# A mixture-of-experts kernel: each place gets a room of tokens in steps of 4 beside its slots in steps of 32

## The chip, the cores and the metric

The kernel runs on one core of one Trainium2 chip. The metric is the time on the device in microseconds (us); less is better. The engines are called as the profile calls them: PE is TensorE's matmul stream and PEld its weight loads, DVE is VectorE, ACT is ScalarE, POOL is GpSimd, SP is SyncE, whose queue issues most of the plain DMAs. L1387 is line 1387 of the kernel before.

## The reference, cut to what matters

There are 16 x 128 = 2048 tokens of width 512. The kernel computes one attention block and one mixture-of-experts block, each with a layer norm ahead and a residual behind. The change is in the second:

```python
x = x + xattn(layernorm(x), ctx, ctx)
h = layernorm(x).reshape(2048, 512)
tidx, tw = gate(h, gate_weight, e_bias)      # 8 of 32 experts for each token, and their weights
comb = zeros(2048, 32).at[rows, tidx].set(tw)
g = einsum('td,eid->tei', h, w1)             # up products, 256 wide per expert
u = einsum('td,eid->tei', h, w3)
a = silu(g) * u
routed = einsum('tei,edi,te->td', a, w2, comb)
shared = (silu(h @ sw1.T) * (h @ sw3.T)) @ sw2.T
out = x + routed + shared
```

The 2048 x 8 = 16384 pairs of a token and an expert are not spread evenly over the experts, and which tokens go where is known only on the chip.

## The kernel before

All products are in fp32; each of the program's matmuls on fp32 data shows as two MATMUL instructions in the profile. The work goes through three stages.

**Attention** (`attention_small`, until about 130 us) ends with the layer norm, the rows of normalized tokens in DRAM (`rows`) and the gate's logits.

**Routing** (`route`, then `slot_tokens`, until about 232 us) picks eight experts per token on DVE, counts the tokens of each expert, and gives each expert a rank by its count (rank 0 has most). Beside it PE computes the shared expert (L250, L1269). Each rank owns a *place*, a fixed stretch of slots of the length `CAPS[rank]`, in steps of 32 slots: 704 for rank 0 down to 448 for rank 31, 17664 slots in all, that is 138 slices of 128. `ORDER` says which rank's place comes at which position, `begins` where each place starts. A token's slot is the place's beginning plus its running number among the expert's tokens, which matmuls on fp16 zeros and ones add up in PSUM (`rank`). Where a place begins and how long it is enter these matmuls as differences to the neighbouring rank: `rise`, made on DVE at L1122 and L1125 from a small table `ranked` that POOL's memsets fill, is multiplied with `behind`, a 32 x 32 table of which rank is ahead of which. From this come `end_p` (L1192), `cap` (L1195) and `limit` (L1211); a token beyond its place's `limit` gets no slot. `flags` compares the counts with the lengths of the places and sets `more` if any expert has more tokens than its place takes. In that case, after the normal work, `rest()` runs every expert over all tokens and adds what was left out.

**Experts** (from about 232 us to the end) works through the 32 places in the order of their positions. A place with more than 512 slots, and the first and last place, is cut into two *pieces*; there are 52. For each piece PE computes the up products (`up`, L1387): two halves of the 256 rows, two weights (w1 and w3), four chunks of the 512 inputs, so 16 products over as many columns as the piece has slots. ACT applies silu (L1396) and DVE the product (L1398) into `acts` (`sa` in the profile). For each slice of 128 slots,

- `gather` (L1351, POOL) fetches the token rows from `rows` with an indirect DMA, five slices ahead,
- `turn` transposes them on PE (L1365), copies them on ACT to `xnT` (L1367), and picks the weights on DVE (L1372),
- `down` multiplies with w2 on PE (L1441), and ACT scales the result into `yw` (L1450),
- `send` (L1413, POOL) adds the rows to the output with an indirect DMA; slots without a token have a number out of bounds and are left out. The first `send` of a place waits until the last one of the place before has landed.

The order on PE, DVE, ACT and POOL is the order of the program, written out by hand: a piece has four steps of up products, and turns and downs of other slices lie between them. The weights of a place (three loads of 512 KB on SP's queue) are in one of three buffers, and are loaded once the place that used the buffer before is done.

The width of an up product is set in `up`:

```python
k, first, end = pieces[n]
m = end - first
```

Of the kernel before, what the change touches and what calls it, by code (L numbers as in the profile page):

```python
# [10 lines left out]
F16 = mybir.dt.float16  # L11
I32 = mybir.dt.int32
AF = mybir.ActivationFunctionType
ALU = mybir.AluOpType
# [4 lines left out]
P = 128  # L19
# [7 lines left out]
TOPK = 8  # L27
NW = 3


CAPS = (
    [704, 672] + [640] * 3 + [608] * 6 + [576] + [544] * 6 + [512] * 7 + [480] * 5 + [448] * 2
# [2 lines left out]
ORDER = [18, 0, 11, 1, 29, 2, 3, 4]  # L35
ORDER += [r for k in range(6) for r in (5 + k, 12 + k)]
ORDER += [*range(19, 29), 30, 31]
BIG = 32768
# [5 lines left out]
def tile_xattn_moe(  # L44
# [15 lines left out]
    nc = tc.nc  # L60
    B, S, D = x.shape
    E, _, ND, I = w1.shape
# [7 lines left out]
    begins = [sum(CAPS[r] for r in ORDER[:k]) for k in range(E + 1)]  # L70
# [71 lines left out]
    not_small = const.tile([1, 1], I32, name="not_small")  # L142
# [7 lines left out]
    limit = const.tile([P, E], F32, name="limit")  # L150

    more = const.tile([1, 1], I32, name="more")
# [802 lines left out]
    def experts(ups, in_order, later, products):  # L955
# [15 lines left out]
        ranked = wp.tile([E, 2, E + 1], F32, name="ranked")  # L971
        rank_at = wp.tile([E, E], F32, name="rank_at")
        for k in range(E + 1):
            r = min(k, E - 1)
            nc.gpsimd.memset(ranked[:, 0, k : k + 1], float(begin_of[r]))
            nc.gpsimd.memset(ranked[:, 1, k : k + 1], float(CAPS[r]))
        for k in range(E):
            nc.gpsimd.memset(rank_at[:, k : k + 1], float(ORDER[k]))

# [46 lines left out]
        def up_matmuls(n):  # L1026
            for _ in range(n):
                next(matmuls, None)

        def route():  # L1030
# [4 lines left out]
            def new(shape, name, dtype=F32, home=None):  # L1035
                return rt.tile(shape, dtype, tag=home or name, name=name)
# [64 lines left out]
            for t in range(NT):  # L1101
                nc.vector.max(t8[:, t, :], ms[:, t, :])
                nc.vector.match_replace(rp[:, t, :], t8[:, t, :], ms[:, t, :], LOWEST)
                if t == NT // 2:
                    product1()
                if t == NT // 2 + 1:


                    ranked_p = new([E, 4], "ranked_p")
                    diag = new([E, E], "diag")  # L1110
                    for i in range(4):
                        nc.vector.scalar_tensor_tensor(
                            diag,
                            ranked[:, i // 2, i % 2 : i % 2 + E],
                            1.0,
                            ident[0:E, 0:E],
                            ALU.mult,
                            ALU.mult,
                            accum_out=ranked_p[:, i : i + 1],
                        )  # L1120
                    rise = new([E, 3], "rise", F16)
                    nc.vector.tensor_tensor(  # L1122
                        rise[:, 0:2], ranked_p[:, 1::2], ranked_p[:, 0::2], ALU.subtract
                    )
                    nc.vector.tensor_tensor(rise[:, 2:3], rise[:, 0:1], rise[:, 1:2], ALU.add)  # L1125
            sel = new([P, NT, E], "sel", F16)
            nc.vector.tensor_tensor(sel, rp, ms, ALU.is_lt)
            comb = new([P, NT, E], "sf")
# [5 lines left out]
            for b in range(NT):  # L1134
                nc.tensor.matmul(
                    count_p,
                    lhsT=sel[:, b, :],
                    rhs=ones[:, 0:1],
                    start=(b == 0),
                    stop=(b == NT - 1),  # L1140
                )
            for b in range(NT):
                nc.tensor.matmul(
                    count,
                    lhsT=ones,
                    rhs=sel[:, b, :],
                    start=(b == 0),
                    stop=(b == NT - 1),
# [17 lines left out]
            for b in range(NT - 1):  # L1166
                nc.tensor.matmul(
                    rank[:, b + 1 :, :],
                    lhsT=ones,
                    rhs=sel[:, b : b + 1, :].to_broadcast([P, NT - 1 - b, E]),  # L1170
                    start=False,
                    stop=False,
                )
                if b == 3:
# [4 lines left out]
                        place, lhsT=ones[0:E, 0:E], rhs=less, start=True, stop=True  # L1179
                    )  # L1180
            behind = new([E, E], "behind", F16)
# [4 lines left out]
                lhsT=rise[:, 0:1].to_broadcast([E, P]),  # L1186
                rhs=behind.unsqueeze(1).to_broadcast([E, NT, E]),
                start=False,
                stop=True,
            )  # L1190
            end_p, cap = small2[:, E : 2 * E], small2[:, 2 * E : 3 * E]
            nc.tensor.matmul(  # L1192
                end_p, lhsT=rise[:, 2:3].to_broadcast([E, P]), rhs=behind, start=True, stop=True
            )
            nc.tensor.matmul(  # L1195
                cap, lhsT=rise[:, 1:2].to_broadcast([E, P]), rhs=behind, start=True, stop=True
            )
# [10 lines left out]
            owner_p = small2[:, 3 * E : 4 * E]  # L1208
            nc.tensor.matmul(owner_p, lhsT=expert_p, rhs=here, start=True, stop=True)
            up_matmuls(4)  # L1210
            nc.vector.tensor_scalar(limit, end_p, float(CAPS[0] - BIG), None, ALU.add)  # L1211
            own = new([P, NT, E], "own", F16, home="eq")
            nc.vector.tensor_tensor(
                own, rank, limit.unsqueeze(1).to_broadcast([P, NT, E]), ALU.is_lt
# [24 lines left out]
            def flags():  # L1239

                over = new([1, E], "over")
                nc.vector.tensor_copy(over, count[0:1])
                nc.vector.tensor_tensor(over, over, cap[0:1], ALU.subtract)
                most = new([1, 1], "most")
                nc.vector.tensor_reduce(most, over, AX.X, ALU.max)
                nc.vector.scalar_tensor_tensor(
                    more, most, float(CAPS[0]), not_small, ALU.is_gt, ALU.max
                )
                nc.vector.tensor_tensor(owner2, owner[:, 1:], owner[:, : E - 1], ALU.subtract)
                nc.vector.tensor_tensor(owner2, owner2, in_next, ALU.mult)  # L1250
                nc.vector.tensor_tensor(owner2, owner2, owner[:, : E - 1], ALU.add)
# [26 lines left out]
        def add_down(b, y):  # L1278
            nc.vector.tensor_tensor(xs[b], y, xs[b], ALU.add)
            nc.sync.dma_start(out[b], xs[b])  # L1280

        sr, sq, weights, flags = route()
        downs = iter(range(B))
        held = []
# [46 lines left out]
        for k in range(E):  # L1331
            first, end = begins[k], begins[k + 1]
# [46 lines left out]
                )  # L1379

        def up(n, i, w, banks):
            k, first, end = pieces[n]
            m = end - first
            pool = (ps_gu, ps_gu2)[i]
            acc = banks[w] = pool.tile([P, TB], F32, tag="gu", name="gu")
            for d in range(ND):
                nc.tensor.matmul(  # L1387
                    acc[:, 0:m],
                    lhsT=wup[k % NW][:, w, d, ts(i, P)],
                    rhs=xnT[n % NTB][:, d, 0:m],  # L1390
                    start=(d == 0),
                    stop=(d == ND - 1),
                )
            if w == 0:
                banks[2] = tp.tile([P, TB], F32, tag="sl", name="sl")
                nc.scalar.activation(banks[2][:, 0:m], acc[:, 0:m], AF.Silu)  # L1396
            else:
                nc.vector.tensor_tensor(  # L1398
                    acts[n % NTB][:, i, 0:m], banks[2][:, 0:m], acc[:, 0:m], ALU.mult
                )  # L1400
# [85 lines left out]
        for n in range(len(pieces)):  # L1486
            tasks = []
            whole = slices_of(n - 1)[1] if n else 0
            needed = slices_of(n + 1)[0] if n + 1 < len(pieces) else NS
            downs_left = list(range(n_down, whole))  # L1490
            turns_left = needed - n_turned
            n_down = whole
            banks = {}
            for step in range(4):
                up(n, step // 2, step % 2, banks)
                left = 4 - step
                for _ in range(-(-turns_left // left)):
                    turn_next()
                    turns_left -= 1
                for _ in range(-(-len(downs_left) // left)):  # L1500
                    down(downs_left.pop(0))
# [7 lines left out]
    pieces = [(k, i) for k in range(NTB) for i in range(NI)]  # L1509
    left_over = attention_small()  # L1510
    experts(pieces[1:], in_order, *left_over)
    left = nc.values_load(
        more[0:1, 0:1],
# [63 lines left out]
```

## Time and profile before

| | |
|---|---|
| median of 3 runs | 1022.8 us (1021.6 to 1024.35) |
| the profiled execution | 1022.55 us, its span 1020.8 us |
| PE busy | 996.8 us, 98% of the span |
| ACT, DVE, POOL busy | 326.2, 254.3, 513.1 us |
| up products (L1387) | 1664 MATMULs, first at 232.6 us |
| down products (L1441) | 672 MATMULs, 260.1 us busy |
| transposes (L1365) | 552 MATMULs, 82.9 us busy |
| granted TensorE clock | 0.995 |
| data moved | 137.06 MB, 134 GB/s in the mean |

The profile is one execution, recorded by the hardware. Matmuls overlap in PE's pipeline, so that the duration of one is longer than the time from its start to the start of the next; what a product costs a busy PE is read from starts. Idle time of an engine that doesn't set the pace costs nothing. A row of a group reads: line, engine, operation, output <- inputs, shapes and count, then busy us and mean ns of one, then the engine's idle time before it and what ended that.

### The profile page before, as it was taken

What the parts mean: (1) busy time and instruction counts of PE and PEld (TensorE: products, weight loads), DVE (VectorE), ACT (ScalarE), POOL (GpSimd) and SP (SyncE); (2) the same over time, 40 slices, a digit from 0 to 9 for tenths busy, and PEclk for the clock granted to TensorE, in tenths of its full rate; (3) what the DMA queues carried; (4) which work ended last, traced back from release to release, by engine and by line L of the source; (5) the groups of instructions that cost most, each with busy time, mean ns of one, the idle gap of its engine ahead of it and who ended that gap; (6) DMA issues with size and microseconds to landing.
All of it is one profiled execution on the core that took longest, in us unless ns stands there. A gap on an engine that the chain in (4) does not pass through costs nothing.

```text
span 1020.8 us, 12451 instructions
## 1 busy us (share of the span) xinstructions
PE 996.8 (98%) x4176; PEld 574.3 (56%) x4176; DVE 254.3 (25%) x902; ACT 326.2 (32%) x517; POOL 513.1 (50%) x658
## 2 busy tenths in 40 slices
PE   8999998999999999999999999999999999999996
PEld 5344444547566556676767676666654444444453
DVE  8887668961011001011111111111111000101000
ACT  5666612422322232232323232323222222222221
POOL 5588633754445444454545454545463444455443
PEclk9999999999999999999999999999999999999998
DMA  9011104135656657775757575757575767565633
GB/s 306 8 43 53 53 22 185 53 112 163 154 137 151 155 133 164 165 164 126 186 126 186 125 185 125 184 127 181 131 176 121 167 173 172 138 146 139 125 66 45
DMA packets 59864, 137.06 MB, mean 134 GB/s; under 512 B 12168, under 2 KB 16392, under 8 KB 59792
## 3 DMA queue, kind: packets, MB, share of 16 engines
q0 software_dynamic: 32032, 69.25, 35.5%
q1 hardware_dynamic: 27680, 66.81, 19.4%
q8 instruction: 35, 0.57, 0.2%
q14 instruction: 37, 0.30, 0.1%
q10 hardware_dynamic: 80, 0.13, 0.0%
HBM read 96.71 MB, written 46.73 MB: 141 GB/s over the span
## 4 chain that ended last, share of the span: by engine, by line
PE 77%; POOL 9%; issue 7%; DVE 4%; DMA 2%; ACT 1%; POOLq 0%; DVEq 0%; ACTq 0%
PE gu L1387 44%; PE y L1441 21%; PE trx L1365 6%; PE gu L250 3%; POOL hq L935 2%; POOL out_dram L1413 2%; POOL xn L214 2%; DMA out_dram<-yw,token 1%; POOL x L471 1%; PE sc L426 1%; DVE st L88 1%; POOL kz L347 1%; PE oT L442 1%; DMA xg<-rows,token 0%; DVE oTs L451 0%
## 5 line engine op out<-in xcount | busy, mean ns | idle before, releaser
L1387 PE MATMUL gu<-xnT,wup 128*128 128x256 f32 (+8 forms) x1664 | 501.9, 450 | 2.4 <-ACT xnT L1367 2.4
L1387 PEld LDWEIGHTS gu<-xnT,wup 128*128 128x128 f32 x1664 | 313.1, 190 | 199.9 <-issue 134.1
L1413 POOL DMA_INDIRECT out_dram<-yw,token x150 | 235.8, 1572 | 366.1 <-ACT yw L1450 265.3
L1441 PE MATMUL y<-wdn,sa 128*128 128x512 f32 (+2 forms) x672 | 260.1, 594 | 0.0
L1398 DVE TENSOR_TENSOR sa<-sl,gu 128x256 f32<-128x256 f32 (+8 forms) x104 | 52.9, 508 | 698.1 <-PE gu L1387 687.6
L1351 POOL DMA_INDIRECT xg<-rows,token x138 | 145.8, 1056 | 48.4 <-issue 32.0
L1450 ACT ACTIVATE yw<-y,wt 128x512 f32<-128x512 f32 x138 | 94.9, 687 | 179.0 <-PE y L1441 154.9
L1441 PEld LDWEIGHTS y<-wdn,sa 128*128 128x128 f32 (+2 forms) x672 | 92.4, 171 | 72.7 <-issue 71.0
L1367 ACT COPY xnT<-trx 128x512 f32<-128x512 f32 (+3 forms) x150 | 81.5, 551 | 142.7 <-PE trx L1365 140.9
L1396 ACT ACTIVATE sl<-gu 128x256 f32<-128x256 f32 (+8 forms) x104 | 47.2, 454 | 247.7 <-PE gu L1387 245.5
L1365 PEld LDWEIGHTS trx<-ident,xg 128*128 128x128 f32 x552 | 69.0, 141 | 37.8 <-issue 26.2
L1365 PE MATMUL trx<-ident,xg 128*128 128x128 f32 x552 | 82.9, 273 | 0.5 <-DMA xg<-rows,token 0.5
L436 ACT ACTIVATE p<-sc 128x1024 f32<-128x1024 f32 x64 | 62.1, 1021 | 28.4 <-PE sc L426 28.4
L250 PE MATMUL gu<-xnT,sup 128*128 128x512 f32 x128 | 59.5, 602 | 2.5 <-DVE sa L261 1.7
L935 POOL TENSOR_SCALAR hq<-slice_q,sq 128x138 f16<-128x138 f16 x32 | 35.2, 1113 | 40.8 <-DVE sq L1235 24.6
L426 PE MATMUL sc<-qT,kz 32*128 32x512 f32 x256 | 41.6, 639 | 1.2 <-DVE qT L417 0.9
L250 PEld LDWEIGHTS gu<-xnT,sup 128*128 128x128 f32 x128 | 22.7, 190 | 26.0 <-issue 20.9
L442 PE MATMUL oT<-p,va 128*32 128x512 f32 x256 | 34.1, 605 | 1.1 <-DVE oTs L451 1.1
L471 POOL TENSOR_TENSOR x<-x,at 128x256 f32<-128x256 f32 x32 | 23.5, 736 | 21.3 <-DVE at L464 21.3
L1372 DVE SCALAR_TENSOR_TENSOR own<-expert,owner,xg 128x32 f32<-128x32 f32 x138 | 31.7, 246 | 1.5 <-DMA xg<-rows,token 1.4
L933 ACT ACTIVATE ht<-hr,token 128x1024 f16<-128x1024 f16 x16 | 18.4, 1147 | 34.4 <-DVE hr L926 34.4
L1269 PE MATMUL y<-sdn,sa 128*128 128x512 f32 x64 | 29.3, 595 | 0.0
(178 smaller groups left out, 467.5 us busy)
## 6 DMA issues: line engine op xcount, KB each, us to landing
wup<-in_w_dram SPq DMA_DIRECT2D x64, 512.0 KB, 5.4
wdn<-in_w_dram SPq DMA_DIRECT2D x32, 512.0 KB, 4.4
rows<-xn SPq DMA_DIRECT2D x16, 256.0 KB, 2.0
out_dram<-x SPq DMA_DIRECT2D x16, 256.0 KB, 2.0
x<-in_x_dram SPq DMA_DIRECT2D x15, 256.0 KB, 5.8
out_dram<-yw,token POOLq DMA_INDIRECT x150, 4.9
xg<-rows,token POOLq DMA_INDIRECT x138, 4.4
cTs<-in_cT_dram SPq DMA_DIRECT2D x4, 256.0 KB, 4.8
```

The costliest lines, as they stand in the source:

```text
L250: nc.tensor.matmul(acc, lhsT=sup[:, w, d, ts(i, P)], rhs=xnT[k][:, d, :], start=(d == 0), stop=(d == ND - 1),)
L426: nc.tensor.matmul(scs[j // 2][:, j % 2], lhsT=kzs[b // 4 % 2][rows, b % 4, i, :], rhs=qTs[b][rows], start=True, stop=True, tile_position= ...
L436: nc.scalar.activation(p, sc, AF.Exp, scale=1.0 / HD**0.5)
L935: engine(k).tensor_scalar(hq[:, k, :], tile_q, sq[:, b, k : k + 1], None, ALU.is_equal)
L1351: nc.gpsimd.indirect_dma_start(out=t, out_offset=None, in_=rows[:, :], in_offset=bass.IndirectOffsetOnAxis(ap=token[:, j : j + 1], axis=0) ...
L1365: nc.tensor.transpose(tr[:, d, :], t[:, ts(d, P)], ident)
L1367: nc.scalar.copy(xnT[n % NTB][:, :, col : col + b - a], tr[:, :, a:b])
L1387: nc.tensor.matmul(acc[:, 0:m], lhsT=wup[k % NW][:, w, d, ts(i, P)], rhs=xnT[n % NTB][:, d, 0:m], start=(d == 0), stop=(d == ND - 1),)
L1398: nc.vector.tensor_tensor(acts[n % NTB][:, i, 0:m], banks[2][:, 0:m], acc[:, 0:m], ALU.mult)
L1413: ins = nc.gpsimd.indirect_dma_start(out=flat, out_offset=bass.IndirectOffsetOnAxis(ap=token2[:, k - 1 : k] if a else token[0:b, j : j + 1 ...
L1441: nc.tensor.matmul(y[c0:c1, :], lhsT=acts[n % NTB][:, i, col : col + c1 - c0], rhs=wdn[pieces[n][0] % NW][:, i, :], start=(i == 0), stop=( ...
L1450: nc.scalar.activation(yws[j], y, AF.Copy, scale=wt[:, j : j + 1])
```

## The change

Beside `CAPS` there is a second list, `ROOM`, with one number for each rank in steps of 4; it is nowhere above `CAPS`. The slots, their slices and the places' beginnings stay as they were. What changes:

- A place takes no more than `ROOM[rank]` tokens: `ranked`, `limit` and the comparison in `flags` use ROOM where they used CAPS.
- The sum of a beginning and a room is no longer a multiple of 32, so `end_p` is made by two matmuls that add up in PSUM, one with the beginnings' differences and one with the rooms'; `rise` loses its third column and the DVE instruction that made it.
- In `up`, the width of the products, of the silu and of the product on DVE ends at the place's room. Columns of `acts` beyond it keep what an earlier piece left there; they belong to slots that have no token.

```diff
+ROOM = [704, 660, 640, 628, 616, 608, 604, 600, 596, 584, 580, 560, 544, 540, 540, 536]
+ROOM += [528, 520, 512, 512, 508, 500, 496, 492, 488, 480, 480, 472, 464, 460, 448, 440]
 
 CAPS = (
     [704, 672] + [640] * 3 + [608] * 6 + [576] + [544] * 6 + [512] * 7 + [480] * 5 + [448] * 2
...
-            nc.gpsimd.memset(ranked[:, 1, k : k + 1], float(CAPS[r]))
+            nc.gpsimd.memset(ranked[:, 1, k : k + 1], float(ROOM[r]))
...
-                    rise = new([E, 3], "rise", F16)
+                    rise = new([E, 2], "rise", F16)
                     nc.vector.tensor_tensor(
-                        rise[:, 0:2], ranked_p[:, 1::2], ranked_p[:, 0::2], ALU.subtract
+                        rise, ranked_p[:, 1::2], ranked_p[:, 0::2], ALU.subtract
                     )
-                    nc.vector.tensor_tensor(rise[:, 2:3], rise[:, 0:1], rise[:, 1:2], ALU.add)
...
-            nc.tensor.matmul(
-                end_p, lhsT=rise[:, 2:3].to_broadcast([E, P]), rhs=behind, start=True, stop=True
-            )
+            for i in range(2):
+                nc.tensor.matmul(
+                    end_p,
+                    lhsT=rise[:, i : i + 1].to_broadcast([E, P]),
+                    rhs=behind,
+                    start=(i == 0),
+                    stop=(i == 1),
+                )
...
-            nc.vector.tensor_scalar(limit, end_p, float(CAPS[0] - BIG), None, ALU.add)
+            nc.vector.tensor_scalar(limit, end_p, float(ROOM[0] - BIG), None, ALU.add)
...
-                    more, most, float(CAPS[0]), not_small, ALU.is_gt, ALU.max
+                    more, most, float(ROOM[0]), not_small, ALU.is_gt, ALU.max
...
         def up(n, i, w, banks):
             k, first, end = pieces[n]
-            m = end - first
+            m = min(end, begins[k] + ROOM[ORDER[k]]) - first
```

## The prediction

> **What bounds it now.** I began with the page's first two parts, to see which engine fills the span, and went on to the chain of waits, to see whether that engine also sets the end:
>
> ```profile
> PE 996.8 (98%) x4176; PEld 574.3 (56%) x4176; DVE 254.3 (25%) x902; ACT 326.2 (32%) x517; POOL 513.1 (50%) x658
> PEclk9999999999999999999999999999999999999998
> PE 77%; POOL 9%; issue 7%; DVE 4%; DMA 2%; ACT 1%; POOLq 0%; DVEq 0%; ACTq 0%
> L1387 PE MATMUL gu<-xnT,wup 128*128 128x256 f32 (+8 forms) x1664 | 501.9, 450 | 2.4 <-ACT xnT L1367 2.4
> ```
>
> TensorE (PE) is busy 98% of the span at a granted clock of 0.995, the chain is 77% PE, and the up products of L1387, which the change shortens, are the largest group: 501.9 us, with 2.4 us of waiting ahead of them in all. Busy PE can hide slack, so next come windows of the expert stage (columns: PE, PEld, DVE, ACT, POOL busy, clock, DMA share, GB/s):
>
> ```profile
> 400.00:500.00 100.00, 100.00 (x404) 67.24 (x403) 10.50 (x54) 28.68 (x52) 47.69 (x36) 1.00 0.67 151
> 500.00:600.00 100.00, 100.00 (x417) 67.50 (x416) 9.95 (x53) 29.39 (x54) 49.17 (x38) 1.00 0.67 154
> 700.00:800.00 100.00, 98.65 (x349) 56.56 (x348) 9.80 (x51) 27.51 (x48) 45.66 (x36) 1.00 0.67 159
> ```
>
> No other engine is over half full, DMA is two thirds full. Last, PE's timeline, to get the true price of one column, since a mean of 450 ns includes the overlapped latency of pipelined matmuls:
>
> ```profile
> 704.44 1.89 PE L1387 MATMUL gu<-xnT,wup 128*128 128x256 f32 x8
> 706.17 0.60 PE L1365 MATMUL trx<-ident,xg 128*128 128x128 f32 x4
> ...
> 711.13 1.88 PE L1441 MATMUL y<-wdn,sa 128*128 128x512 f32 x4
> 712.85 2.53 PE L1387 MATMUL gu<-xnT,wup 128*128 128x352 f32 x8
> 715.22 0.60 PE L1365 MATMUL trx<-ident,xg 128*128 128x128 f32 x4
> ```
>
> Read from start to start: eight of 256 columns take 706.17 - 704.44 = 1.73 us, 216 ns each; eight of 352 take 715.22 - 712.85 = 2.37 us, 296 ns each. The difference is 80 ns for 96 columns: **0.833 ns per column and instruction**, and some 3 ns fixed. This is the stream of a full pipeline: less columns, the next instruction starts earlier.
>
> **What the Trainium skill says.** "TensorE: Matmul & The Clock Gate", section "Wait — 56ns, not 53.3ns?", gives N/2.4 GHz + about 2.5 ns from start to start. "FP8 and Floating Point Precision", section "TensorE Precision Notes", says that true fp32 takes four passes. The code has 52 pieces x 2 halves x 2 weights x 4 = 832 products, the page 1664 MATMULs, so an instruction is two passes: 2 x 256/2.4 + 2.5 = 215.8 ns, against 216 in the trace. Both agree. "SBUF — State Buffer", section "Door 1: The DMA port swizzle", tells of 16-byte lines, four fp32: every new width is a multiple of 4, so none ends within one. No run here shows that effect, nor any width that isn't a multiple of 32.
>
> **Up products.** CAPS minus ROOM, by rank, is 12 (rank 1), 12, 24 (3, 4), 4, 8, 12, 24, 28, 16 (6 to 11), 4, 4, 8, 16, 24 (13 to 17), 4, 12, 16, 20, 24 (20 to 24), 8, 16, 20 (27 to 29) and 8 (31): 324 columns in 23 places; the other nine lose none. 17664 columns become 17340. The cut falls on a place's last piece only. A piece has 16 products, so 32 instructions: 324 x 32 x 0.833 ns = **8.64 us less PE**. Instructions, weight loads and their order stay the same. The narrowest cut piece has 232 columns, 196 ns an instruction. Is the weight load (190 ns each in its row) then the floor? The uncut piece of 192 columns answers:
>
> ```profile
> 985.73 1.46 PE L1387 MATMUL gu<-xnT,wup 128*128 128x192 f32 x8
> 987.03 0.60 PE L1365 MATMUL trx<-ident,xg 128*128 128x128 f32 x4
> ```
>
> 1.30 us for eight, 162.5 ns each, below 190 ns, so loads overlap and 232 is safe.
>
> **Silu and product** (L1396, L1398) shrink too: by the shape rows, (597 - 384)/256 = 0.83 ns a column on ACT, (688 - 421)/256 = 1.04 on DVE, twice per piece: 0.5 and 0.7 us. I count zero: ACT and DVE wait on PE there; if that cover were gone, it would still be a gain.
>
> **Routing.** One small tensor_tensor (L1125) leaves DVE, one matmul joins PE:
>
> ```profile
> 153.51 0.15 DVE L1122 TENSOR_TENSOR rise<-ranked_p 32x2 f16<-32x2 f32 x1
> 153.69 0.15 DVE L1125 TENSOR_TENSOR rise<-rise 32x1 f16<-32x1 f16 x1
> ...
> 161.84 0.17 PE L1192 MATMUL places<-behind,rise 32*128 32x32 f16 x1
> 161.87 0.17 PE L1195 MATMUL places<-behind,rise 32*128 32x32 f16 x1
> 161.89 0.17 PE L1209 MATMUL places<-here,expert_p 32*128 32x32 f16 x1
> ```
>
> DVE's top-8 loop follows L1125, and PE idles 2.1 us for `sel` after it, so it is on the path: -0.18 us (start to start). The matmul costs about 0.03 us by its neighbours; `limit` on DVE waits for the group. Net -0.15 us; bounds -0.2 and +0.2, if a matmul's whole 0.17 us showed. The memsets of ROOM for CAPS are one for one. SP's and POOL's queues keep every instruction in the same place.
>
> **Moved and late next.** Slots, slices, gathers (138), scatters (150), transposes, down products and weight loads stay at 32-step sizes. What must keep up with PE is POOL. A place has 4.3 gathers (1.06 us and 0.3 of issue) and 4.7 scatters (1.57 and 0.3), and once a landing (4.9 us median): 5.8 + 8.8 + 4.9 = 19.5 us, where PE takes (1011 - 233)/32 = 24.3 us and will take 24.0. In the waits POOL's scatters stand 265.3 us for `yw`, so for PE, and 44.7 us for landings. That cover holds 4.5 us per place; the change uses 0.27. At the end the chain runs along POOL from 959.9 us; if POOL alone paced that stretch, the cuts of its places (at most 16 + 8 + 8 columns) would be lost: 0.85 us. But the last scatters wait for `yw`:
>
> ```profile
> 1010.58 1.56 POOL L1413 DMA_INDIRECT out_dram<-yw,token  x1 [2.02 <-ACT yw L1450]
> ```
>
> So I count them.
>
> **Sum.** -8.64 - 0.15 = -8.8 us against the profiled execution: span 1020.8 to 1012.0, its time (1.75 us around the span) 1022.55 to 1013.75. The median of the runs, 1022.8, lies 0.25 above: **1014.0 us**.
>
> **Rivals.**
> 1. *Widths are rounded up.* The trace has only multiples of 32. Rounded to 16, 176 columns remain cut: 4.7 us, 1018.1. Rounded to 32, none: 1022.7, no change. For it: no row shows another width. Against: one slope and one small constant fit 192, 256, 288 (1.94 us for eight) and 352. Chance 6%, split evenly.
> 2. *The gain is absorbed*: scatters, or a landing at a change of places, become the pace. By the 19.5 against 24.0 us this needs a place to shrink by 4.5 us; a few bad places might cost 2 to 4 us, 1016 to 1018. Chance 6%.
> 3. *Slower: an expert overflows its room.* ROOM replaces CAPS in `flags` (L1244) too; one count over its rank's room sets `more`, and `rest()` runs all tokens through all experts: 32 x (64 x 2 up + 64 down instructions) x 430 ns (a 512-column step: 1.72 us for four at 711.13) = 2640 us, some 3660 in all. It decides at one token too many. The router of reference.py on its inputs gives sorted counts 652, 649, 631, 609, ... 281; all fit, rank 11 with 560 of 560, ranks 7 to 9 and 17 with one to spare. Disturbing its logits by 3e-5 made no overflow in 200 draws, by 1e-4 one. Chance 2%.
> 4. *Slower: a surcharge on widths off 32.* Spread over 23 x 32 = 736 instructions the gain is 11.7 ns each; beyond that it loses. At 20 ns: 1029. Nothing speaks for it; 1%.
>
> The forecast itself has 85%, 1012 to 1016: the runs before spread 2.75 us.
>
> **Numbers.** Range 1012.0 to 1018.3, through rounding to 16 and absorption. A measurement of this kernel tells 0.3%, 3.1 us, from no change. Faster by more: forecast, absorption, rounding to 16 and nearly no rest, 0.92. Within: rounding to 32 and a larger absorption, 0.05. Slower: 0.03.
>
> **What would show it.** L1387's rows at new widths (232 to 508) must start 0.833 ns a column sooner, e.g. 240 columns at 203 ns, eight in 1.62 us. The group's busy time falls by about 8.6 us, PE stays full in the windows, its first up product stays at 232.6 us within 0.3. It is wrong if a 252-column instruction takes what one of 256 does, if PE's idle time grows by over 2 us, or if instructions of `rest` appear.

## The result and the profile after

The changed kernel takes 1014.01 us in the median of four runs (1011.92 to 1014.39), where before has 1022.2 in these runs: a ratio of 0.9913, 95% interval 0.9896 to 0.9931. The forecast was 1014.0. The agreement to the last digit is partly luck: the sum behind it was right to 0.1 us, but each kernel's own times are spread over 2 to 4 us, for a reason that the prediction missed and the experiments found.

The page of the changed kernel; the up products are now on L1395:

```profile
PE 987.3 (98%) x4177; PEld 574.8 (57%) x4177; DVE 253.3 (25%) x901; ACT 325.8 (32%) x517; POOL 512.7 (51%) x658
...
PE 76%; POOL 10%; issue 7%; DVE 4%; DMA 2%; ACT 0%; POOLq 0%; DVEq 0%; ACTq 0%
...
L1395 PE MATMUL gu<-xnT,wup 128*128 128x256 f32 (+27 forms) x1664 | 493.2, 445 | 2.4 <-ACT xnT L1374 1.7
```

The group has the same 1664 instructions and the same 2.4 us of waiting ahead of them; its busy time fell from 501.9 to 493.2 us. PE has one instruction more and DVE one fewer. Windows of the expert stage (PE, PEld, DVE, ACT, POOL busy, clock, DMA share, GB/s) show PE as full as before:

```profile
500.00:600.00 100.00, 100.00 (x420) 67.78 (x419) 10.53 (x54) 28.63 (x52) 49.60 (x38) 1.00 0.69 157
700.00:800.00 100.00, 98.65 (x348) 56.03 (x347) 9.78 (x50) 27.81 (x49) 47.17 (x37) 1.00 0.65 154
```

And PE's timeline gives the price of one of the new widths:

```profile
685.35 1.78 PE L1395 MATMUL gu<-xnT,wup 128*128 128x240 f32 x8
686.97 1.88 PE L1449 MATMUL y<-wdn,sa 128*128 128x512 f32 x4
...
706.30 2.34 PE L1395 MATMUL gu<-xnT,wup 128*128 128x324 f32 x8
708.48 0.60 PE L1372 MATMUL trx<-ident,xg 128*128 128x128 f32 x4
```

From start to start, eight instructions of 240 columns take 1.62 us and eight of 324 take 2.18 us: 202.5 and 272.5 ns each, a difference of 70 ns for 84 columns, again 0.833 ns a column.

The profiled execution, at 1011.92 us, was the fastest of the four, and its span is 10.7 us shorter than the one of before, not 8.8. Two starts locate the difference. The first up product starts at 230.6 us (before: 232.6), and the last scatter at 1001.8 (before: 1012.4). So the expert stage between them shrank from 779.8 to 771.2 us, by 8.6, and 2.0 us came from ahead of it. Of these, 0.3 us are there when the count matmuls start. Most of the rest arises at one place, the matmuls that add up the ranks. This is PE before:

```profile
156.96 0.55 PE L1135 MATMUL count<-ones,sel 128*32 128x1 f16 x16 [2.14 <-DVE sel L1127]
...
158.21 1.65 PE L1167 MATMUL rank<-sel,ones 128*128 128x480 f16 x4
```

and after:

```profile
156.63 0.55 PE L1137 MATMUL count<-ones,sel 128*32 128x1 f16 x16 [1.96 <-DVE sel L1129]
...
157.74 0.89 PE L1169 MATMUL rank<-sel,ones 128*128 128x480 f16 x4
```

The same four matmuls take 1.65 us in one and 0.89 in the other. Windows of one microsecond in the profile of before say why; the third number from the end is the granted clock:

```profile
157.00:158.00 1.00, 1.00 (x33) 0.94 (x34) 0.63 (x1) 0.00 (x0) 0.00 (x0) 0.96 0.00 0
158.00:159.00 1.00, 1.00 (x5) 0.32 (x3) 0.92 (x4) 0.00 (x0) 0.00 (x0) 0.50 0.00 0
159.00:160.00 1.00, 1.00 (x5) 0.31 (x4) 0.15 (x1) 0.00 (x0) 0.00 (x0) 0.50 0.00 0
160.00:161.00 1.00, 1.00 (x5) 0.59 (x6) 0.83 (x6) 0.00 (x0) 0.00 (x0) 0.50 0.00 0
161.00:162.00 1.00, 1.00 (x13) 0.76 (x11) 0.13 (x1) 0.00 (x0) 0.00 (x0) 0.83 0.00 0
```

After PE has idled for 2.14 us, its clock is at one half for some 3.4 us. In this stretch of the changed kernel's profile it was 1.00 throughout. Is that an effect of the change, or chance? The experiments had to separate it.

### The profile page after: what moved, and what is told of

It is laid out like the page before. It is cut to its first block, busy times and chain, and to the rows that moved or that the text cites. A ratio compares the mean times of both kernels' runs of the same rounds, so it can differ in the third digit from the quotient of the medians.

```text
span 1010.1 us, 12452 instructions
## 1 busy us (share of the span) xinstructions
PE 987.3 (98%) x4177; PEld 574.8 (57%) x4177; DVE 253.3 (25%) x901; ACT 325.8 (32%) x517; POOL 512.7 (51%) x658
## 4 chain that ended last, share of the span: by engine, by line
PE 76%; POOL 10%; issue 7%; DVE 4%; DMA 2%; ACT 0%; POOLq 0%; DVEq 0%; ACTq 0%
PE gu L1395 44%; PE y L1449 21%; PE trx L1372 6%; PE gu L253 3%; POOL hq L938 2%; POOL out_dram L1421 2%; POOL xn L217 2%; POOL x L474 1%; DMA out_dram<-yw,token 1%; DVE st L91 1%; PE warm L325 1%; POOL kz L350 1%; DVE oTs L454 1%; PE sc L429 1%; POOL h L113 0%
## 5 line engine op out<-in xcount | busy, mean ns | idle before, releaser
L1395 PE MATMUL gu<-xnT,wup 128*128 128x256 f32 (+27 forms) x1664 | 493.2, 445 | 2.4 <-ACT xnT L1374 1.7
L1395 PEld LDWEIGHTS gu<-xnT,wup 128*128 128x128 f32 x1664 | 313.1, 190 | 193.0 <-issue 132.6
L1406 DVE TENSOR_TENSOR sa<-sl,gu 128x256 f32<-128x256 f32 (+27 forms) x104 | 52.2, 502 | 690.3 <-PE gu L1395 672.0
L1404 ACT ACTIVATE sl<-gu 128x256 f32<-128x256 f32 (+27 forms) x104 | 46.7, 449 | 240.5 <-PE gu L1395 234.2
```

The source lines that it names most:

```text
L1395: nc.tensor.matmul(acc[:, 0:m], lhsT=wup[k % NW][:, w, d, ts(i, P)], rhs=xnT[n % NTB][:, d, 0:m], start=(d == 0), stop=(d == ND - 1),)
L1406: nc.vector.tensor_tensor(acts[n % NTB][:, i, 0:m], banks[2][:, 0:m], acc[:, 0:m], ALU.mult)
```

## The experiments

**Each kernel's spread.** The changed kernel as it is, in more runs.

> The changed kernel again, for more runs of both. Theory A (PE's stream alone): the difference to before is -8.64 us from the up products and -0.15 us from the routing, so a median of 8 to 9 us below before. Theory B (the clock): in the profile of before TensorE's clock stood at 0.50 from about 158 to 161.4 us and cost about 1.7 us, after an idle gap of 2.14 us ahead of the count matmuls; in the changed kernel's profile the gap was 1.96 us and the clock stayed at 1.00. If that drop comes in some executions and not in others, the times of each kernel lie in two heaps about 2 us apart (about 1012 and 1014 for the changed kernel, 1021 and 1023 for before).

Measured: 1014.81 us in the median (1012.93 to 1015.51, six runs) against 1023.03 for before (1020.96 to 1025.42, 27 runs), ratio 0.9918 (0.99 to 0.9935). The times follow the mean clock of their run, but only roughly: the ten runs of before with 0.997 average 1021.35 us, the eight with 0.995 average 1023.41, the five with 0.993 average 1024.51, while the other four, with 0.994 and 0.996, lie out of that order at 1023.77 to 1025.42; the changed kernel has 1012.93 at 0.998 and 1015.33 and 1015.51 at 0.994. The profiles show the drop to half the clock in both kernels. In this one's profile it came, from about 157.5 to 160.9 us, although the gap was 1.96 us, as in the first profile without a drop. Its first up product started at 233.0, its last scatter at 1004.2: the stage again took 771.2 us.

**Widths alone.** The kernel before, with the list ROOM and one line:

```diff
-            m = end - first
+            m = min(end, begins[k] + ROOM[ORDER[k]]) - first
```

> Only the widths in up end at the room; the routing is that of before (places take CAPS tokens, one end_p matmul, the DVE instruction kept). Theory A: -8.64 us of the -8.8, so about 1013.7 where before has 1022.3. Rival (the routing carries part of the gain, about 2 us, because its shorter gap keeps the clock up): about -6.7 us, near 1015.5, with the clock at 0.50 after the gap in its profile.

Measured: 1014.34 us, ratio 0.9913 (0.9893 to 0.9932), the full gain within the intervals. From the first up product to the last scatter its profile has 232.8 to 1004.0, 771.2 us. This profile has the drop (a clock of 0.81 between 156 and 165 us), as the rival expected, and still the stage has the whole 8.6 us. The rival, that the routing carries 2 us of the gain, fails.

**Routing alone.** The changed kernel with the old width, `m = end - first`.

> Only the routing is changed (room in ranked, limit and flags, two end_p matmuls, no third column of rise); the up products keep the full width of the places. Theory A: -0.15 us, no difference that can be told from before. Rival: -2 us, if the gap that is 0.18 us shorter keeps the clock at 1.00 in most runs.

Measured: 1022.01 us, ratio 0.999 (0.9982 to 0.9999), which is 1.0 us less with an interval of 0.1 to 1.8: it excludes the rival's 2 us, and includes the 0.15. Runs with an equal mean clock are the closer comparison: eight with 0.997 average 1021.13, where the ten of before average 1021.35, 0.2 us less (0.1 if the two with 0.998 are counted in). The profiled execution shows how far chance reaches: the clock averaged 0.66 between 156 and 165 us and 0.94 in the five us after, its first up product came at 234.8, and it took 1024.71. But its expert stage took 779.8 us (234.8 to 1014.6), as before. Its drop is twice as long as the one in the profile of before, some 6.8 us:

```profile
158.00:159.00 1.00, 1.00 (x7) 0.43 (x6) 0.96 (x4) 0.00 (x0) 0.00 (x0) 0.91 0.00 0
159.00:165.00 6.00, 6.00 (x21) 3.15 (x21) 4.34 (x28) 0.59 (x1) 0.00 (x0) 0.50 0.00 0
165.00:166.00 1.00, 1.00 (x3) 0.53 (x2) 0.90 (x6) 0.00 (x0) 0.00 (x0) 0.68 0.51 82
```

The drop behind this gap has one of these two lengths, 3.4 or 6.8 us, in all eight profiles that show it. At half the clock that costs a busy PE 1.7 or 3.4 us. By this estimate the times of before should lie in three heaps, near 1021.3, 1023.0 and 1024.7; they do so roughly, but only a profile shows the clock of a single stretch.

**Odd widths.** One column more in each of the 23 cut pieces.

```diff
-            m = min(end, begins[k] + ROOM[ORDER[k]]) - first
+            m = min(end, begins[k] + ROOM[ORDER[k]] + 1) - first
```

> The changed kernel with one column more in each of the 23 cut pieces: widths are odd (233 to 509), so none is a multiple of 4. Linear theory (0.833 ns a column at any width): +0.61 us, and eight instructions of 241 columns start 1.63 us apart. Rival (widths are rounded up to 4, 8 or 16 or carry a surcharge when they end within a 16-byte line): 244 or 248 columns' time, 1.65 to 1.68 us for eight, or a surcharge of 10 ns on 736 instructions, +7 us.

The single time, 1016.52 us, says little, since the clock stood at 0.64 between 156 and 165 us. The stage is clean: 234.6 to 1006.4, 771.8 us, 0.6 more than the changed kernel, as the straight line gives. And the rows:

```profile
689.68 1.79 PE L1395 MATMUL gu<-xnT,wup 128*128 128x241 f32 x8
691.31 1.88 PE L1449 MATMUL y<-wdn,sa 128*128 128x512 f32 x4
```

1.63 us for eight of 241 columns, one column's worth more than for 240. There is no rounding up and no surcharge. The 16-byte lines of the Trainium skill's "SBUF — State Buffer", section "Door 1: The DMA port swizzle", which the prediction cited as a reason for trust in multiples of 4, show no effect in it.

**How far the line goes.** All widths at three quarters, then at half; the columns beyond are not computed.

```diff
             m = min(end, begins[k] + ROOM[ORDER[k]]) - first
+            m = m * 3 // 16 * 4
```

> All widths cut to three quarters (12968 columns for 17340): a quarter of the slots gets no new up product, so that part of the computation is left out. Slots, gathers, scatters and down products stay. Linear theory: 4372 columns x 32 x 0.833 ns = -116.6 us against the changed kernel, about 897: PE takes 20.5 us per place, still above POOL's 19.5. Rival (POOL's scatters and landings pace already): 20 to 60 us of it are lost, 920 to 955, and PE idles behind transposes or yw.

Measured: 895.02 us; the stage took 652.1 us (232.8 to 884.9), 119.1 less than the changed kernel's, for 116.6 from the line. Of the other 2.5 us PE's waits explain 1.9 (1.5 us in all for 3.4 in the changed kernel's second profile). All of the line's gain arrives, 13 times the change's.

```diff
             m = min(end, begins[k] + ROOM[ORDER[k]]) - first
+            m = m // 8 * 4
```

> All widths cut to half (8648 columns): half of the slots get no new up product, that part is left out. Linear theory: -231.8 us, about 782, 17 us per place. Theory of the prediction (POOL's 19.5 us per place is the next bound): the expert stage doesn't fall below 32 x 19.5 = 624 us, so about 867, with POOL without idle time and PE waiting. A third outcome: widths of 96 to 256 columns stop at the time of a weight load (190 ns each, if they didn't overlap): PE stays busy, the start-to-start time of the narrow instructions stays at 110 to 190 ns, and the time lies between 782 and 870.

Measured: 817.17 us, the stage 576.3 us (230.7 to 807.0): 194.9 of the 231.8 arrive. The time lies in the range of the third outcome, but PE does not stay busy, as that one asks, and the 867 us of the prediction's floor is undercut. In the waits of that stage (engine, line and what it waited for, us in total, times, longest)

```profile
ACT yw L1459 <- DMA out_dram<-yw,token: 133.9, 54, 6.2
...
POOL out_dram L1422 <- DMA out_dram<-yw,token: 44.7, 14, 4.9
...
PE y L1450 <- DVE sa L1407: 12.0, 5, 3.7
```

ACT stands for one of the four buffers of `yw` to be scattered, and PE idles 28.9 us (548.4 busy of 577.3; in the changed kernel's stage 768.3 of 771.2). The clock adds to it: it fell to 0.50 at three of PE's gaps in this stage, of 3.41, 3.65 and 2.79 us, for 13.6 us in all. PE was busy for some 12 us of that, so an estimate of its cost is 6 us. POOL is not full, at 374.2 us busy, so it was not POOL's own work that set the pace. The narrowest products also leave the line:

```profile
499.29 1.05 PE L1396 MATMUL gu<-xnT,wup 128*128 128x128 f32 x8
500.18 0.60 PE L1372 MATMUL trx<-ident,xg 128*128 128x128 f32 x4
...
779.37 1.03 PE L1396 MATMUL gu<-xnT,wup 128*128 128x96 f32 x8
780.23 0.60 PE L1372 MATMUL trx<-ident,xg 128*128 128x128 f32 x4
```

Eight of 128 columns take 0.89 us, 111 ns each, about what the line gives (109.6). Eight of 96 take 0.86 us, 107.5 ns each, where it gives 83. Some longer rows of 128 columns take more (16 in 2.04 us), for a reason that was not found. What share of the missing 36.9 us belongs to the buffers, the clock and the narrow products was not tried apart.

**An overflow.** One step off the fullest room.

```diff
-... 596, 584, 580, 560, 544, 540, 540, 536]
+... 596, 584, 580, 556, 544, 540, 540, 536]
```

> The room of rank 11 is 556 for 560, one step of 4 less. If the counts on the chip are those of the reference's router, rank 11 has 560 tokens, four are left for rest(), and the time is about 1014 + 2640 = 3660 us. If the counts on the chip differ so that rank 11 has 556 or fewer, 1014.

Measured: 3723.36 us. Rank 11 does have more than 556 tokens on the chip, and the rival's price was right to 3%. `rest` is there in two groups that no other kernel has:

```profile
L871 PE MATMUL gu<-xnT,up 128*128 128x512 f32 x4096 | 1780.5, 593 | 3.9 <-ACTq L904 3.9
L884 PE MATMUL y<-dn,a 128*128 128x512 f32 x2048 | 932.9, 599 | 0.4 <-DVE a L880 0.4
```

**The clock, first try.** Two of the shared expert's products moved ahead of the gap.

```diff
-            up_matmuls(20)
+            up_matmuls(22)
```

> The changed kernel with two more of the shared expert's up products (four instructions of 430 ns, 1.72 us) ahead of the count matmuls, taken from later: up_matmuls(20) becomes up_matmuls(22). The idle gap should shrink from 1.96 to about 0.24 us. Theory B: the clock never drops there, all times lie in the lower heap, about 1012, and the median is 1 to 2 us below the changed kernel's. Rival (the drop has nothing to do with the gap, or the two products are missed later as cover): no difference, or up to 1.7 us slower.

Measured: 1012.99 us (1012.79 to 1014.79, five runs), ratio 0.9901 (0.9883 to 0.992), 1.8 us below the changed kernel in the same comparison. The gap shrank to 0.25 us and the clock stayed at 1.00 behind it. But the two products are missed later, and in the profiled run, the slowest of the five, the clock dropped there instead:

```profile
156.00:160.00 4.00, 3.75 (x52) 2.31 (x51) 3.34 (x13) 0.00 (x0) 0.00 (x0) 1.00 0.00 0
160.00:165.00 5.00, 5.00 (x16) 2.34 (x15) 4.43 (x28) 0.59 (x1) 0.15 (x1) 1.00 0.15 40
165.00:170.00 5.00, 2.78 (x5) 1.05 (x4) 5.00 (x15) 2.78 (x3) 4.64 (x4) 0.79 0.99 370
```

PE was busy for only 2.78 of the five us from 165. So the theory and its rival were each half right: the gap moved, to 2.22 us ahead of these two products.

**The clock, second try.** The gap is filled with products on zeros that nobody needs.

```diff
+            warm = ps_y.tile([P, D], F32, tag="y", name="y")
+            for _ in range(8):
+                nc.tensor.matmul(warm[:, 0:P], lhsT=wz, rhs=wz, start=True, stop=True)
             small = ps_sm.tile([P, 512], F32, tag="small", name="count")
```

> The changed kernel with eight extra products on zeros (16 instructions of 128 columns, about 1.75 us) ahead of the count matmuls, into a bank of y that nobody reads; the shared expert's products stay where they are. The gap should shrink from 1.96 to about 0.2 us and, unlike in e7_fill, none opens later. Clock theory: the drop after the gap never comes, nearly all times lie at 1012 to 1013, 1.5 to 2 us below the changed kernel's median. Rival (zeros don't count as work for the clock, or the drop comes from something else): times spread as before, 1012 to 1015.5.

> The same eight products in the kernel before. Clock theory: nearly all times at 1021 to 1021.5, where before has a second heap at 1023 to 1025; the difference between e9_warmb and e8_warm is then the change without the clock's share, 8.6 to 8.8 us by the widths and the DVE instruction. Rival: the spread stays, or the difference is 2 us off that.

> The changed kernel once more on this chip, to be compared with e8_warm and e9_warmb: 1014 to 1015 in the median, times between 1012 and 1015.5, lower where the mean clock is higher.

Measured on one chip: 1012.43 us for the changed kernel with the fill (1012.31 to 1012.77, four runs; ratio to before 0.9906, 0.9891 to 0.9921), 1013.09 without (1012.16 to 1013.86, four runs, below the 1014 to 1015 expected), and 1021.21 for before with the fill (1020.87 to 1021.55 in 21 runs, where before itself went from 1020.97 to 1024.9). The spread goes to a sixth. The profile of the filled kernel shows the gap closed:

```profile
154.76 1.95 PE L1136 MATMUL y<-wz 128*128 128x128 f32 x16
156.88 0.55 PE L1140 MATMUL count<-ones,sel 128*32 128x1 f16 x16 [0.17 <-DVE sel L1129]
```

The profiles of both filled kernels have a clock of 1.00 from 156 to 170 us. With the clock's share out of both, the change itself is worth 1021.21 - 1012.43 = **8.78 us**, where the runs of each kernel lie within 0.7 us. Their stages differ by 8.6 (231.3 to 1011.1 against 231.1 to 1002.2). The filled kernel's four runs lie within 0.5 us, but that its median is lower than that of the changed kernel, 1012.43 for 1013.09, is not clear with four runs of each.

## Why the prediction was right, and where it was not

- **What bounds it.** Right: PE's stream. Its windows stay full, and a column less is 0.833 ns less, at 240 and 324 columns, at odd widths, and in the halved kernel down to about 128 columns.
- **Up products, -8.64 us.** The stage between the first up product and the last scatter shrank by 8.6 us: it took 771.2 us in all six profiles with the new widths (three of the changed kernel, the widths alone and the two fills) and 779.8 in the three with the old ones (before, the routing alone, before with the fill). So the clock ahead of it plays no part in it. Nothing was lost at POOL's tail; the 0.85 us that could have gone there did not.
- **Routing, -0.15 us.** The DVE instruction was worth what its starts said: `rise` to the next step of the top-8 loop took 0.26 us before and takes 0.08, and the gap ahead of the count matmuls fell from 2.14 to 1.96 us. The filled pair (8.78 for 8.8) and the routing-only runs of equal clock (-0.1 to -0.2) agree with the net, though neither resolves 0.15 us.
- **The first up product at 232.6 us, within 0.3.** Wrong: it came at 230.6 in the first profile, and in those of other kernels at up to 234.8. The step that failed is the first reading, in which a mean clock of 0.995 and a row of nines were taken for an even clock. The trace of before had the drop: a window from 156 to 165 us would have shown 0.81. So the prediction set its sum against an execution with a drop and treated the runs' 2.75 us as mere spread. The median hid this, since by their times most runs of the changed kernel had a drop too.
- **Late next.** The size was off. A place was given 19.5 us on POOL, with a landing of 4.9 us; halved widths ran at 18.0 us per place, and POOL's waits for landings were 44.7 us in 14 cases, 1.4 us per place. The landing mostly lies beside other work. What came late first, by the waits, was a free buffer of `yw`, on ACT, and it did not matter at 13 times the change's cut, but did at 27 times.
- **Rivals.** Rounding and surcharge are refuted by the odd widths. Absorption is refuted by three quarters of the width, where all of the gain arrives. The overflow is real and costs some 2709 us beside the changed kernel's 1014, where 2640 were worked out; with ROOM at 560 for a rank of 557 to 560 tokens it just doesn't come for these inputs.

Left open: whether the 0.18 us shorter gap makes the drop rarer. With the new routing 15 of 36 runs lie in the lowest heap (four of the changed kernel's 14 below 1013 us, eleven of the routing-only 22 below 1022), with the old one 21 of before's 57 (below 1022). That tells nothing either way. What decides whether a given execution has the drop is open too.

## What to carry to other kernels

When one engine is full and the change shortens its stream, price it from start to start of instructions in the timeline, times the exact number of instructions: this sum held to 0.1 us of 8.6 in the stage. Look at the clock in windows of a few microseconds around each idle gap of PE before comparing two profiles, and compare stages, not spans: here a gap of 2 us ahead of small matmuls moved the start of the next stage by 2 to 4 us. Where moving work only moves such a gap, as it did here, matmuls on zeros that nobody waits for can close it.

## What the runs showed of the hardware

- The clock fell to 0.50 after a PE gap of only 2 us, in some executions and not in others: at the gap of 1.96 to 2.14 us ahead of the count matmuls in eight of ten profiles, six times for 3.4 us and twice for 6.8. Matmuls of one column behind the gap are not needed for it: with the two products moved it fell behind a gap of 2.22 us followed by products of 512 columns. At the gap of 1.70 to 1.73 us near 137 us it fell in none of 13 profiles, and at one of 2.60 us in the halved kernel it did not either. The Trainium skill's "TensorE: Matmul & The Clock Gate", section "Part 1: The HAM clock gate (the "warmup" mystery)", names the half rate and a free-running window of about 3.4 us, which agrees with the two lengths. It puts the drop after at least one idle window, which is longer than these gaps of 2 us.
- Products on zeros count as work for that clock: with eight of them in the gap the 21 runs of before spread over 0.7 us, where 25 without them spread over 4.
- The width of an fp32 product costs the same 0.833 ns a column whether or not it is a multiple of 4, down to about 128 columns (111 ns for 109.6 by the line). Below that it gets hardly shorter: 107.5 ns at 96 columns, where the line gives 83.
